# First group's two sets on raw, transposed x, with the normalisation put in afterwards

## The chip, the core and the metric

The kernel runs on one core of a Trainium2 chip. The metric is the device time of one execution in microseconds. The engines are TensorE (PE in the profile; PEld is its weight load), VectorE (DVE), ScalarE (ACT), GpSimd (POOL) and SyncE (SP, which issues nearly all DMAs). All arithmetic is in 32-bit floats.

## The reference

With `x` of 2 x 1024 tokens by 512 features:

```
xn  = (x - mean(x)) / sqrt(var(x) + 1e-5)                  # per token
s   = xn @ (weight * blockmask).T                          # 512 x 512, 32 x 32 blocks
nx  = xn * rsqrt(mean(xn^2) + 1e-5) * ln_w
ffn = (silu(nx @ gate.T) * (nx @ up.T)) @ down.T           # 1792 hidden features
out = x + s * silu(ffn)
```

## The kernel before

Tokens are split into four tiles of 512 (t = 0 to 3), the 512 features into four chunks of 128 (c = 0 to 3). The matrix products are done by a two-level recursive scheme (seven products in place of eight, on each level). On the outer level a group g of gate and up columns has seven sets q; its two first sets, q = 1 and q = 2, multiply the plain blocks of the weights (feature halves K = 0 and 1) by the plain blocks of token tiles 0 and 1. The program's `order` lists first q = 1 and 2 of every group (g = 0 to 7, where group 7 is the masked linear layer), then the other five sets of every group. Position j in this list numbers a set: j = 0 and 1 are group 0's two, j = 2 and 3 group 1's. The down projection follows with a similar scheme.

Each set is one call of `instance`: seven products, m = 1, 5, 2, 6, 3, 7, 4 in order of issue, each a 128x128 by 128x512 matmul (two records in the trace). Products 1, 2 and 3 take token blocks as they are, 5, 6, 7 and 4 take differences of token blocks, which `inner_b` makes: with b11, b12, b21, b22 for (chunk, tile) they are t5 = b12 - b11, t6 = b22 - t5, t7 = b22 - b12, t4 = b21 - t6. `inner_a` makes the sums of weight blocks on POOL, after `scale_a` has multiplied a weight tile by `ln_w`. Products accumulate in three kinds of PSUM banks, X (three banks), Y (two) and Z (one); a fourth kind, V (two), serves everything else: idle products, transposes, gate values, held copies. Banks of a kind are used in turn. Between products, a bank's running value is copied out (`snap`, `seed`, `total`): by ACT in a group's first set, by DVE with an addition of the first set's sums (`prior`) in its second. From j = 2 on a set is `seeded`: ACT copies X into the Z bank before product 2 accumulates there.

All instructions are put into one list with `at(pos, ...)` and issued in the order of `pos`; every engine carries out its own in that order. One position is one product slot, 7 per set; `T(us)` turns a planned time into a position. `plan` puts in a list of steps. The times in the program only set the order.

At the head, `load_x` loads x by tokens, `stats` and `factors` make each token's scale and shift, `normalise` applies them (ACT and DVE, in halves of 256 columns), `transpose` turns each 128x128 piece on TensorE into a V, X or Y bank, and `evacuate` copies it out. Products of set 0 need the transposed pieces of tile 0, the differences those of tile 1. Meanwhile `warm` runs 22 idle products on the identity. Tiles 2 and 3 are done otherwise, later: `load_xt` loads x already transposed (`x_t`), `fac_rows` turns the factors into rows through TensorE, writes them to DRAM and reads them back over all partitions, and `scale_xt` applies them on POOL.

`group` has where a group's sums go: `acc` for set 1's, `c1` for set 2's; when two halves of c1 are complete, `silu` (ACT) and `h_out` (DVE) make the gated product, and later an SP transfer stores the `acc` sums to DRAM.

Of the kernel before, what the change touches and what calls it, by code (L numbers as in the profile page):

```python
# [31 lines left out]
def tile_masked_linear_gated_ffn(  # L32
# [22 lines left out]
    fac_dram = tc.dram_tile([2, 2, W], F32, name="fac_dram")  # L55
# [51 lines left out]
    blockones = const.tile([P, P], F32, tag="blockones", name="blockones")  # L107
    keep = const.tile([P, 4, 16], F32, tag="keep", name="keep")

    def constants():  # L110
        nc.gpsimd.memset(eps2, EPS * EPS)
        make_identity(nc, ident)
        nc.scalar.activation(stat_0, eps2, AF.Sqrt)
        nc.gpsimd.memset(blockones, 0.0)
        for b in range(P // BLK):
            nc.gpsimd.memset(blockones[b * BLK : (b + 1) * BLK, b * BLK : (b + 1) * BLK], 1.0)
# [4 lines left out]
    fac = small.tile([P, 2, 2, TT], F32, tag="fac", name="fac", bufs=1)  # L121
    rms = small.tile([P, NTT, TT], F32, tag="rms", name="rms", bufs=1)

    def load_x(t):
        for i in range(TT):
            xt[t, i] = mem[:, first_slot[("B6", "vc", "v5", "B4")[t]] + i, :]
            nc.sync.dma_start(xt[t, i], x[(t * TT + i) * P : (t * TT + i + 1) * P, :])
# [6 lines left out]
    def factors(t, i=0, n=TT):  # L134


        if t < 2:
            scl = small.tile([P, n], F32, tag="scl", name=f"scl_{t}_{i}", bufs=3)
            nb = small.tile([P, n], F32, tag="nb", name=f"nb_{t}_{i}", bufs=3)
        else:  # L140
            scl, nb = fac[:, t - 2, 0, :], fac[:, t - 2, 1, :]
        for k in range(n):
            stat[t, i + k] = (scl[:, k : k + 1], nb[:, k : k + 1])
        rows = slice(i, i + n)

        def last():
            nc.vector.reciprocal(scl, scl)
            nc.vector.scalar_tensor_tensor(nb, agg[:, t, rows, 0], -1.0, scl, ALU.mult, ALU.mult)

        return [lambda: nc.scalar.activation(scl, agg[:, t, rows, 1], AF.Sqrt, bias=eps2, scale=1.0 + EPS), last]  # L150
# [60 lines left out]
    def fac_rows(t):  # L211
        b = bank("V", f"fac_rows_{t}")
        nc.tensor.transpose(b[: 2 * TT, :P], fac[:, t - 2].rearrange("p f i -> p (f i)"), ident)
        rows = small.tile([2 * TT, P], F32, tag="rows", name=f"fac_sb_{t}")
        nc.scalar.copy(rows, b[: 2 * TT, :P])
        nc.sync.dma_start(fac_dram[t - 2].rearrange("f (i p) -> (f i) p", p=P), rows)
        for f in range(2):
            fac_bc[t, f] = mem[:, F["B6"] + 3 + 2 * (t - 2) + f, :]
            nc.sync.dma_start(fac_bc[t, f], fac_dram[t - 2, f].unsqueeze(0).to_broadcast([P, W]))

    def scale_xt(t, c, f):
        v = u12[c, t % 2] if c < 2 else raw[c, t]
        add(pool, v, v, fac_bc[t, f], (ALU.mult, ALU.add)[f])

# [160 lines left out]
    def instance(j, g, q, prior, dest, after):  # L385
# [4 lines left out]
        seeded = j > 1  # L390

        def mm(m, tag, key, first):
            if first and key not in st:
                st[key] = bank("Y" if key == "z" and j == 1 else tag, f"{key}_{j}")
            nc.tensor.matmul(st[key], weights(g, q, m), operand(q, m), start=first and not (key == "z" and seeded),  # L395
                             stop=True, skip_group_check=True)

        def seed():

            if seeded:  # L400
                st["z"] = bank("Z", f"z_{j}")
                nc.scalar.copy(st["z"], st["x"])  # L402
            else:
                st["s1"] = slot("s2" if j else "s5", f"s1_{j}")
                if prior is None:
                    nc.scalar.copy(st["s1"], st["x"])
                else:
                    add(dve, st["s1"], st["x"], prior(0))
# [19 lines left out]
        for off, m, tag, first, snapshot, out in (  # L428
# [9 lines left out]
            at(EARLY.get((j, m), pos), mm, m, tag, key, first)  # L438
            if snapshot:
                at(pos + 1, snap, key, *snapshot)  # L440
            elif out:

                pos += 2.3 if prior is None and m == 2 and seeded else 1
                if m == 2:
                    pos = EARLY.get((j, "z"), pos)
                at(pos, total, key, *out)
# [3 lines left out]
    def group(g, where):  # L450
# [5 lines left out]
        h11 = tiles(F["a1"])  # L456
        gate = {}
# [14 lines left out]
        def done(R, Hh, tiles):  # L472
# [3 lines left out]
            def after(i, pos):  # L476
# [5 lines left out]
                if n in ready and n + 2 in ready:  # L482
                    key = (R, Hh, n)
                    p = max(ready[n] + 1.2, ready[n + 2] - 0.5, SILU)
# [5 lines left out]
        def summed(dst, src, into, then=None, engines=(pool,) * 4):  # L490
# [9 lines left out]
            1: (None, acc, nothing),  # L500
            2: (acc, c1, done(0, 0, c1)),
# [16 lines left out]
        at(7 * where[g, 1] + 15, lambda: nc.sync.dma_start(acc_dram[g], sums))  # L518
# [117 lines left out]
    def down_instance(o, q, where_, prior, dest, after):  # L636
# [78 lines left out]
        if last_set:  # L715
            at(where_(17) + 0.1, base_of_last)
            for part, pos in zip(parts, (where_(23), where_(24), where_(25))):
# [12 lines left out]
    EARLY.update({(0, 1): T(10.4), (0, 2): T(11.3), (1, 1): T(12.1), (1, 2): T(13.0), (0, 0): T(11.5), (1, 0): 4.3,  # L730
                  (0, "z"): 2.2, (1, "z"): 4.5})
    SILU = 26.2
    at(T(-10), constants)
    at(T(-10), load_x, 0)
    at(T(-10), lambda: nc.scalar.dma_start(lnw_sb, ln_w))

    at(T(-10), lambda: nc.gpsimd.tensor_copy(mem[:, F["a1"], 0:1], xt[0, 0][:, 0:1]))
    at(T(-10), load_a, 0, 0)
    at(T(-10), load_x, 1)
    at(T(-10), load_a, 0, 1)  # L740

    at(T(9.95), lambda: nc.gpsimd.memset(mem[:, F["a1"] + 2, 0:1], 0.0))
    for K in range(2):
        at(T(9.96), load_a, 1, K)
    at(T(9.96), load_x, 2)
    for K in range(2):
        at(T(9.96), load_a, 2, K)
    at(T(9.96), load_x, 3)
# [8 lines left out]

    at(T(1.4), lambda: warm(22, bank("V", "idle")))
    plan(T(4.9), 0, factors(0, 0, 2))
    plan(T(7.1), 0, factors(0, 2, 2))  # L760
    for t, p, step in ((1, T(12.5), 0), (3, 23.2, 0.6), (2, 36.1, 1.2)):
        plan(p, step, factors(t))
    for us, i, h in ((5.9, 0, 0), (6.0, 0, 1), (6.1, 1, 0), (7.2, 1, 1), (7.95, 2, 0), (8.4, 2, 1), (7.95, 3, 0), (8.4, 3, 1)):
        at(T(us), normalise, 0, i, dve if i == 3 else act, slice(h * W // 2, (h + 1) * W // 2))
    for i in range(TT):
        half = act if i < 2 else dve
        at(T(3.7 + 0.82 * i), stats, 0, i)
        at(T(9.35 + 0.82 * i), stats, 1, i)
        for h, cols in enumerate((slice(0, W // 2), slice(W // 2, W))):
            at(T(13.45 + 0.9 * h + 0.4 * (i % 2)), normalise, 1, i, half, cols)  # L770
        for c in range(KC):
            at(T((8.9, 9.3, 9.8, 11.0)[c] + 0.05 * i), transpose, 0, c, (0, 1, 3, 2)[i], "XYYX"[c])
            at((T(14.35), T(14.8), T(15.25), 4.1)[c] + 0.06 * i, transpose, 1, c, (2, 3, 0, 1)[i], "XVVV"[c])
    at(T(6.0), scale_a, 0, 0, pool)
    at(T(10.0), scale_a, 0, 1, pool)
    for c in range(KC):
        at(T((9.75, 10.3, 10.85, 12.05)[c]), evacuate, 0, c, act)
        at((5.6, 2.09, 6.0, 5.05)[c], evacuate, 1, c, act)
    for pos, q, m, eng in ((1.1, 1, 5, dve), (1.87, 1, 6, dve), (2.56, 1, 7, dve), (3.95, 2, 5, dve), (2.7, 1, 4, pool),
                           (5.06, 2, 6, dve), (10.05, 2, 7, dve), (5.07, 2, 4, pool)):  # L780
        at(pos, inner_b, q, m, eng)
    for q in (1, 2):
        for k in (0, 1):
            for n in (0, 1):
                at(8, outer_b, q, k, n, None)
    at(5.1, scale_a, 1, 0)
    at(5.2, scale_a, 1, 1)
    for i in range(TT):
        at(14.0 + 2.5 * i, stats, 3, i)
# [5 lines left out]
    at(25.2, fac_rows, 3)  # L795
    at(40.8, fac_rows, 2)
    for n, p0 in ((1, 31), (0, 50)):
# [3 lines left out]
    for k in (0, 1):  # L801
        at(37 + 1.5 * k, outer_b, 7, k, 1, pool)
        at(43 + 1.5 * k, outer_b, 6, k, 1, pool)
# [19 lines left out]
    for g in range(G + 1):  # L823
# [8 lines left out]
        if g:  # L832
            plan(p - 7, 1, inner_a(g, 1))
        else:
            plan(T(9.9), 0, inner_a(0, 1, 0, 1))
            plan(2.75, 0, inner_a(0, 1, 1, 1))
# [150 lines left out]
```

## Time and profile before

| | |
|---|---|
| median of 3 runs | 506.8 us (506.78 to 507.37) |
| the profiled execution | 506.61 us, span 504.8 us |
| TensorE busy | 499.2 us (99%) |
| VectorE busy | 375.6 us (74%) |
| ScalarE busy | 188.1 us (37%) |
| GpSimd busy | 358.8 us (71%) |
| DMA | 124.75 MB, mean 247 GB/s |

All times of a row are in microseconds from the span's start. A row of the view in order of time has the start, the time taken by the rows merged in it, the engine, the line, what is written and read, how many, and in brackets how long the engine sat idle before it and what released it. The chain is found from the end backwards: each instruction is followed to what it waited for. A busy share is an average over the whole span; the head and the rest of the kernel have different limits.

### The profile page before, as it was taken

What the parts mean: (1) busy time and instruction counts of PE and PEld (TensorE: products, weight loads), DVE (VectorE), ACT (ScalarE), POOL (GpSimd) and SP (SyncE); (2) the same over time, 40 slices, a digit from 0 to 9 for tenths busy, and PEclk for the clock granted to TensorE, in tenths of its full rate; (3) what the DMA queues carried; (4) which work ended last, traced back from release to release, by engine and by line L of the source; (5) the groups of instructions that cost most, each with busy time, mean ns of one, the idle gap of its engine ahead of it and who ended that gap; (6) DMA issues with size and microseconds to landing.
All of it is one profiled execution on the core that took longest, in us unless ns stands there. A gap on an engine that the chain in (4) does not pass through costs nothing.

```text
span 504.8 us, 4923 instructions
## 1 busy us (share of the span) xinstructions
PE 499.2 (99%) x1231; PEld 227.4 (45%) x1231; DVE 375.6 (74%) x578; ACT 188.1 (37%) x362; POOL 358.8 (71%) x301
## 2 busy tenths in 40 slices
PE   8999999999999999999999999999999999999996
PEld 7444444444444444444444444444444444444444
DVE  6887887876968969697896969879657644377636
ACT  6667775734535363443535333330101101001111
POOL 5629997464886959879696999985672764649960
PEclk9999999999999999999999999999999999999999
DMA  6878746368178594876949475599996798467362
GB/s 208 306 234 335 292 168 250 123 251 293 62 245 295 186 329 181 295 240 244 335 154 317 179 265 213 216 351 387 365 335 221 253 389 311 130 238 269 106 229 84
DMA packets 62221, 124.75 MB, mean 247 GB/s; under 512 B 5968, under 2 KB 13552, under 8 KB 60144
## 3 DMA queue, kind: packets, MB, share of 16 engines
q1 hardware_dynamic: 62048, 124.43, 69.1%
q8 instruction: 10, 0.16, 0.1%
q14 instruction: 19, 0.16, 0.1%
q10 hardware_dynamic: 144, 0.00, 0.0%
HBM read 78.25 MB, written 46.15 MB: 246 GB/s over the span
## 4 chain that ended last, share of the span: by engine, by line
PE 97%; DVE 1%; ACT 1%; DMA 1%; issue 0%; DVEq 0%; ACTq 0%
PE x L395 38%; PE y L395 19%; PE dx L643 15%; PE z L395 10%; PE dy L643 8%; PE dz L643 5%; PE dv L643 1%; PE pt L165 1%; DMA mem<-in_x 1%; DVE mem L98 0%; ACT mem L158 0%; DVE st L131 0%; DVE mem L633 0%; ACT silu L626 0%; ACT scl L150 0%
## 5 line engine op out<-in xcount | busy, mean ns | idle before, releaser
L98 POOL TENSOR_TENSOR mem<-mem 128x512 f32<-128x512 f32 (+4 forms) x261 | 322.1, 1257 | 111.6 <-ACT mem L423 30.5
L395 PE MATMUL x<-mem 128*128 128x512 f32 x448 | 211.7, 593 | 0.0
L395 PEld LDWEIGHTS x<-mem 128*128 128x128 f32 x448 | 84.6, 190 | 107.3 <-issue 89.7
L98 DVE TENSOR_TENSOR mem<-x,mem 128x512 f32<-128x512 f32 x137 | 93.4, 686 | 42.1 <-PE x L395 40.4
L395 PE MATMUL y<-mem 128*128 128x512 f32 x224 | 114.6, 593 | 0.1
L643 PE MATMUL dx<-mem 128*128 128x512 f32 x174 | 78.3, 592 | 0.0
L98 DVE TENSOR_TENSOR mem<-mem 128x1536 f32<-128x1536 f32 (+3 forms) x50 | 66.9, 1342 | 6.9 <-PE dx L643 4.4
L98 DVE TENSOR_TENSOR mem<-y,mem 128x512 f32<-128x512 f32 x96 | 65.9, 686 | 7.9 <-PE y L395 6.5
L402 ACT COPY z<-x 128x512 f32<-128x512 f32 x54 | 30.9, 573 | 94.7 <-PE x L395 91.7
L395 PEld LDWEIGHTS y<-mem 128*128 128x128 f32 x224 | 42.2, 190 | 53.1 <-issue 46.5
L395 PE MATMUL z<-mem 128*128 128x512 f32 x112 | 57.3, 593 | 0.0
L643 PEld LDWEIGHTS dx<-mem 128*128 128x128 f32 x174 | 33.1, 190 | 41.6 <-issue 40.9
L643 PE MATMUL dy<-mem 128*128 128x512 f32 x98 | 44.5, 592 | 0.0
L461 ACT ACTIVATE gate<-mem 128x512 f32<-128x512 f32 x56 | 32.7, 602 | 20.4 <-DVE mem L98 15.9
L466 DVE TENSOR_TENSOR mem<-gate,mem 128x512 f32<-128x512 f32 x56 | 38.1, 682 | 1.9 <-ACT gate L461 1.5
L616 POOL TENSOR_TENSOR mem<-mem 128x512 f32<-128x512 f32 x16 | 25.8, 1619 | 13.6 <-DMA mem<-s_dram 13.4
L626 ACT ACTIVATE silu<-mem 128x512 f32<-128x512 f32 x15 | 9.0, 602 | 64.6 <-DVE mem L98 48.3
L395 PEld LDWEIGHTS z<-mem 128*128 128x128 f32 x112 | 21.1, 190 | 25.9 <-issue 21.4
L98 DVE TENSOR_TENSOR mem<-z,mem 128x512 f32<-128x512 f32 x41 | 28.1, 685 | 2.8 <-PE z L395 2.7
L643 PEld LDWEIGHTS dy<-mem 128*128 128x128 f32 x98 | 18.6, 190 | 23.4 <-issue 23.2
L98 DVE TENSOR_TENSOR mem<-dx,mem 128x512 f32<-128x512 f32 x16 | 11.1, 691 | 20.3 <-PE dx L643 20.2
L643 PE MATMUL dz<-mem 128*128 128x512 f32 x56 | 25.2, 592 | 0.0
(86 smaller groups left out, 286.9 us busy)
## 6 DMA issues: line engine op xcount, KB each, us to landing
h_dram<-mem SPq DMA_DIRECT2D x98, 256.0 KB, 2.2
mem<-h_dram SPq DMA_DIRECT2D x28, 768.0 KB, 6.7
mem<-in_gu SPq DMA_DIRECT2D x42, 256.0 KB, 3.9
acc_dram<-mem SPq DMA_DIRECT2D x8, 1024.0 KB, 4.0
mem<-acc_dram SPq DMA_DIRECT2D x8, 1024.0 KB, 6.1
mem<-in_x_t SPq DMA_DIRECT2D x24, 256.0 KB, 5.5
mem<-in_x SPq DMA_DIRECT2D x16, 256.0 KB, 4.5
s_dram<-mem SPq DMA_DIRECT2D x16, 256.0 KB, 6.1
```

The lines of the kernel that those rows point to most:

```text
L98: eng.tensor_tensor(o, a, b, op)
L165: nc.tensor.transpose(pt[t, c][:, i * P : (i + 1) * P], xt[t, i][:, c * P : (c + 1) * P], ident)
L395: nc.tensor.matmul(st[key], weights(g, q, m), operand(q, m), start=first and not (key == "z" and seeded), stop=True, skip_group_check=True)
L402: nc.scalar.copy(st["z"], st["x"])
L461: nc.scalar.activation(gate[key], t(), AF.Silu)
L466: nc.vector.tensor_mul(a(), gate[key], b())
L616: at_later.append(lambda: nc.gpsimd.tensor_tensor(s_tile, s_tile, rms_bc[t], ALU.mult))
L626: nc.scalar.activation(b[0][:, part], y[:, part] if source is None else source(), AF.Silu)
L643: nc.tensor.matmul(st[key], w(), b(), start=first and key != "z", stop=True, skip_group_check=True)
```

## The change

Sets 0 and 1 (group 0, q = 1 and 2) no longer wait for normalised tokens. They multiply raw x, loaded already transposed (`load_rx`); `raw_b` makes their differences, on DVE through a copy in a V bank (`rhold`) or on POOL. Since normalising is a scale and a shift for each token, and a token is a column of the outputs, the outputs are mended: `mend_scale` multiplies by the tokens' scale, `mend_shift` adds the tokens' shift times the sum of the weights over features. These sums are made by `row_sums`, eight products with a column of ones. The factors of tiles 0 and 1 go through `fac_rows` as those of 2 and 3 do; `hold_fac` copies such a tile into a V bank for DVE. Tile 0 and 1 are still normalised and transposed, for group 1 onwards, and what belonged to j = 0 and 1 in the order's early part (the use of tile 1's transposes, the unseeded sets) moves on by 14 positions (S) to j = 2 and 3. Group 0's sums lie in other slots (`acc_1`, `c1` in B3 and B4), its `silu` comes at position 39.5, its store at 53. The number of idle products goes from 22 to 17, loads are issued in another order, and two small POOL instructions that held back weight loads go.

```diff
+    def load_rx(c, t):
+        i = {0: F["B5"] + 3, 1: F["B5"] + 5, 2: F["B5"], 3: F["B7"]}[c] + t
+        rx[c, t] = mem[:, i, :]
+        nc.sync.dma_start(rx[c, t], x_t[c, t])
...
+    def rhold(c):
+        rheld[c] = bank("V", f"rx_{c}")
+        nc.scalar.copy(rheld[c], rx[c, 1])
...
+        if eng is dve:
+            a, b = (rheld[c], rx[c, 0]) if m == 5 else (rheld[c + 1], rop[q, 5])
+        else:
+            a, b = (rx[c + 1, 1], rx[c, 1]) if m == 7 else (rx[c + 1, 0], rop[q, 6])
+        add(eng, o, a, b, ALU.subtract)
+
+    def row_sums():
+        b = bank("V", "row_sums")
+        for K in range(2):
+            for r in range(2):
+                for c in range(2):
+                    nc.tensor.matmul(b[:, 2 * K + r : 2 * K + r + 1], aq[0, 0, K][:, (2 * c + r) * P :][:, :P], ones,
+                                     start=c == 0, stop=c == 1, skip_group_check=True)
+        nc.vector.tensor_copy(rowsum[:, 0, :], b[:, 0:2])
+        nc.vector.tensor_tensor(rowsum[:, 1, :], b[:, 2:4], rowsum[:, 0, :], ALU.add)
...
+    def hold_fac(n, f):
+        fac_held[n, f] = bank("V", f"fac_{n}_{f}")
+        nc.scalar.copy(fac_held[n, f], fac_bc[n, f])
+
+    def mend_scale(v, n, eng):
+        add(eng, v, v, fac_held[n, 0] if eng is dve else fac_bc[n, 0], ALU.mult)
+
+    def mend_shift(v, k, r, n):
+        nc.vector.scalar_tensor_tensor(v, fac_held[n, 1], rowsum[:, k, r : r + 1], v, ALU.mult, ALU.add)
...
-        seeded = j > 1
+        seeded = j > 3
...
+            nc.tensor.matmul(st[key], weights(g, q, m), rop[q, m] if j < 2 else operand(q, m), start=first and not (key == "z" and seeded),
...
+            for n in range(2):
+                for r in range(2):
+                    at(23.6 + 1.2 * (2 * n + r), lambda n=n, r=r: mend_scale(c1(2 * r + n), n, pool))
+                    at(34.5 + 2.6 * n + 0.9 * r, lambda n=n, r=r: mend_shift(c1(2 * r + n), 1, r, n))
+                    at(44 + 4.4 * n + 0.9 * r, lambda n=n, r=r: mend_scale(acc_1(2 * r + n), n, dve))
+                    at(46 + 4.4 * n + 0.9 * r, lambda n=n, r=r: mend_shift(acc_1(2 * r + n), 0, r, n))
+                at(33.5 + 2.6 * n, hold_fac, n, 1)
+                at(43 + 4.4 * n, hold_fac, n, 0)
+                at(45 + 4.4 * n, hold_fac, n, 1)
...
-                    p = max(ready[n] + 1.2, ready[n + 2] - 0.5, SILU)
+                    p = max(ready[n] + 1.2, ready[n + 2] - 0.5, SILU if g else 39.5 + 0.5 * n)
...
+    for j, todo in enumerate((
+        {1: 4.9, 2: 5.8, 5: 6.7, 6: 7.6, 3: 8.5, 7: 9.4, 4: 11.1, 0: 6.6, (5, "out"): 7.7, (6, "out"): 8.5, (2, "out"): 9.3,
+         (3, "out"): 10.0, (7, "out"): 10.5, (4, "out"): 12.0},
+        {1: 10.2, 2: 12.0, 5: 12.9, 6: 13.8, 3: 14.7, 7: 15.6, 4: 18.0, 0: 11.1, (5, "out"): 14.55, (6, "out"): 14.8,
+         (2, "out"): 14.1, (3, "out"): 16.2, (7, "out"): 16.4, (4, "out"): 19.0})):
...
-    at(T(-10), load_x, 0)
...
     at(T(-10), load_a, 0, 0)
+    for c, t in ((0, 0), (1, 0), (0, 1), (1, 1)):
+        at(T(-10), load_rx, c, t)
+    at(T(-10), load_x, 0, 0, 2)
+    at(T(-10), load_a, 0, 1)
+    at(T(-10), load_rx, 2, 0)
+    at(T(-10), load_x, 0, 2, 4)
+    for c, t in ((3, 0), (2, 1), (3, 1)):
+        at(T(-10), load_rx, c, t)
+    at(T(-10), load_a, 1, 0)
     at(T(-10), load_x, 1)
+    at(T(-10), load_a, 1, 1)
...
-    at(T(1.4), lambda: warm(22, bank("V", "idle")))
-    plan(T(4.9), 0, factors(0, 0, 2))
-    plan(T(7.1), 0, factors(0, 2, 2))
+    at(T(1.4), lambda: warm(17, bank("V", "idle")))
+    plan(T(9.25), 0, factors(0, 0, 2))
+    plan(T(14.5), 0, factors(0, 2, 2))
...
+    for us, i, h in ((10.5, 0, 0), (10.6, 0, 1), (11.1, 1, 0), (11.2, 1, 1), (15.2, 2, 0), (15.3, 3, 0), (15.35, 2, 1), (15.4, 3, 1)):
+        at(T(us), normalise, 0, i, act, slice(h * W // 2, (h + 1) * W // 2))
...
+            at(T(16.6 if c < 2 else 18.05) + 0.1 * c + 0.01 * i, transpose, 0, c, (0, 1, 3, 2)[i], "VVXX"[c])
+            at((T(14.35), T(14.8), T(15.25), 4.1)[c] + 0.06 * i + S, transpose, 1, c, (2, 3, 0, 1)[i], "XVVV"[c])
+    at(T(3.6), scale_a, 0, 0)
+    at(T(9.1), scale_a, 0, 1)
+    at(T(13.0), scale_a, 1, 0)
+    at(T(17.0), scale_a, 1, 1, pool)
+    for us, c in ((5.6, 0), (6.3, 1), (11.8, 2), (12.5, 3)):
+        at(T(us), rhold, c)
+    for us, q, m, eng in ((6.1, 1, 5, dve), (6.8, 1, 6, dve), (7.0, 1, 7, pool), (8.9, 1, 4, pool), (12.4, 2, 5, dve),
+                          (13.2, 2, 6, dve), (13.3, 2, 7, pool), (15.1, 2, 4, pool)):
+        at(T(us), raw_b, q, m, eng)
+    at(9.6, row_sums)
+    at(5.4, fac_rows, 0)
+    at(15.4, fac_rows, 1)
```

## The prediction

> **What bounds the kernel now.** I read the page first (busy shares and the chain that ended last), then the TensorE and ScalarE rows of the first 30 us in order of time, then busy time by stretch where the change puts its repairs.
>
> ```profile
> PE 499.2 (99%) x1231; PEld 227.4 (45%) x1231; DVE 375.6 (74%) x578; ACT 188.1 (37%) x362; POOL 358.8 (71%) x301
> PE 97%; DVE 1%; ACT 1%; DMA 1%; issue 0%; DVEq 0%; ACTq 0%
> ```
>
> The chain is TensorE at 97%: 392 products of the first phase and then the down phase, at one product per 0.858 us (1.72 us for two in the chain's rows). Time can be won only by starting the stream earlier or by closing gaps in it; any gap that the change opens is lost in full. So the head decides:
>
> ```profile
> 1.37 6.97 PE L756 MATMUL idle<-ident 128*128 128x128 f32 x44 [1.37 <-POOL ident masks.py:199]
> 8.78 1.39 PE L165 MATMUL pt<-ident,mem 128*128 128x128 f32 x10 [0.22 <-DVE mem L156]
> 10.01 1.10 PE L395 MATMUL x<-mem 128*128 128x512 f32 x2
> 14.31 1.47 PE L165 MATMUL pt<-ident,mem 128*128 128x128 f32 x12
> 15.69 1.13 PE L395 MATMUL y<-mem 128*128 128x512 f32 x2
> 22.58 1.02 PE L395 MATMUL y<-mem 128*128 128x512 f32 x2
> ```
>
> The 22 idle products are 44 records and keep TensorE until about 8.06. The first real product starts at 10.01; the one at 22.58 is the twelfth, and from there products follow without a gap. Eleven products are 9.44 us, so 12.57 us hold 3.1 us of something else: 20 transposes at 0.11 (2.2 us) and 0.9 us of gaps. The head is nearly full already.
>
> Two rows show a bank that TensorE waits for:
>
> ```profile
> 14.95 1.49 DVE L98 TENSOR_TENSOR mem<-pt,mem 128x512 f32<-128x512 f32 x2 [0.46 <-PE pt L165]
> 16.47 0.58 ACT L173 COPY mem<-pt 128x512 f32<-128x512 f32 x1 [1.29 <-DVE mem L98]
> 17.11 0.14 PEld L165 LDWEIGHTS pt<-ident,mem 128*128 128x128 f32 x1 [0.26 <-ACT mem L173]
> ```
>
> Two V banks are used in turn. V banks go to the idle products, then to tile 1's chunks c=1, c=2, c=3. So c=3 must wait for the copy of c=1, which ends at 17.05; its weights load at 17.11. Here two products lie ahead of it and hide the wait.
>
> **The change, part by part.** I write (j, m) for product m of set j; sets 0 and 1 are those that now take raw x.
>
> *Start: the gain.* Busy time by half microseconds shows the idle products' pace change near 5.0 to 5.2 us (some 4 records touch a stretch before, 6 to 7 after, though the granted clock reads 1.00 throughout). From there 28 of the 44 records remain, 3.0 us, 0.107 each; the first 16 took 3.7 us. Now there are 17 products, 34 records: 16 before 5.1, then 18 x 0.107 = 1.9, so TensorE is free at 7.0. Is the data there? Ten loads of 256 KB landed between 3.5 (the first) and about 10.05 (the DMA share falls from 0.97 to 0.04 at 10), 0.73 apart. In the new order the weight tile lands first, 3.5; x_t chunks at 4.2, 5.0, 5.7, 6.5; the scaling on ACT takes 0.9, done by 4.6. The idle products end last: (0,1) starts at 7.06, 2.95 earlier than before. [...]
>
> *Sets 0 and 1: a new queue on ACT.* ACT's rows follow program order. Its steps: copy 0.48, scaling one weight tile 0.88, four normalise halves 2.08. A reader of a product starts 1.14 after the product does (10.01 to 11.15). (0,6) is the fourth product, 9.63; its snapshot starts on ACT at 10.77; the second weight tile's scaling is behind it, 11.25 to 12.13. (1,1) needs that and starts at 12.26, (1,2) at 13.98. But ACT then has the square root (0.3), a 0.45 wait for DVE's factors, and four normalise halves, 13.0 to 15.1, before it copies the x_t chunk that (1,5)'s operand is taken from: 15.1 to 15.7. DVE, one statistics pair of 0.82 in its way, subtracts at 16.1 to 16.8. (1,5) starts at 16.85, where TensorE was free at 14.84: **gap 2.0**. ACT goes on: two copies, the next weight tile (to 17.4), the square root that waits for the fourth x tile's statistics (DVE, 18.2), factors, four more halves 19.24 to 21.35. TensorE ends (1,7) at 20.29 and its next work, the transposes of tile 0, needs the halves: **gap 1.2**.
>
> *Row sums and the factor rows.* Eight products with one output column are 16 records. None is in the trace; by the transposes (0.107 a record, the same 128-column weights) 1.7 us, 1.4 by the 0.087 load of the fac_rows row, 3.0 by the 0.19 load of the products. I take 1.7. In the order they stand just ahead of (2,1), so they are on the path; a gain is excluded, since nothing is taken away for them. Two more fac_rows transposes add 0.24. [...]
>
> So: transposes of two chunks 0.9, (1,4) 0.86, two chunks 0.9, factor row and sums 1.8 after 21.45: (2,1) starts at 25.9; four products later, 29.4, tile 1's transposes.
>
> *The bank.* New V banks (two held chunks twice, two transposes, fac_rows of tile 0, row sums) come first, and fac_rows of tile 1 falls between chunks c=1 and c=2. Now c=2 falls on c=1's bank and is queued ahead of (2,5). By the rows above the bank comes free 2.1 after DVE's first subtraction starts (14.95 to 17.05). TensorE has nothing to do meanwhile: transposes end at 30.4, c=2 starts at 32.0, **gap 1.6**, and (2,5) at 32.47. It is the nineteenth product; before, the nineteenth is at 22.58 + 7 x 0.858 = 28.59, and c=3's 0.45 lies behind it only now. The terms: -2.95 (start), +1.3 (twelve transposes that lay ahead of the first product before), +2.0, +1.2, +1.7, +0.2, +1.6, less before's own 0.9 of gaps: +4.2, by the two clocks 32.47 + 0.45 - 28.59 = **+4.3**. [...]
>
> *Repairs on DVE.* Between positions 33 and 52 come 8 shifts and 4 scalings of 128x512 on DVE, 6 copies on ACT, and two gate products are moved there: 14 DVE operations at 0.60 (start to start of full rows) = 8.4 us. The shift's form is not in the trace at this size; the bank-reading row it is nearest to takes 0.68, 0.60 in a stream; half or double are the ends. This is before's 43 to 59 us; the rows give busy time by stretch, in the order TensorE, weight loads, DVE, ACT, POOL:
>
> ```profile
> 46.00:50.00 4.00, 4.00 (x12) 1.75 (x11) 2.33 (x5) 1.95 (x4) 4.00 (x5) 1.00 0.97 372
> 50.00:54.00 4.00, 4.00 (x11) 1.75 (x10) 2.54 (x5) 3.99 (x9) 4.00 (x4) 1.00 0.49 154
> 54.00:58.00 4.00, 4.00 (x10) 1.71 (x9) 3.90 (x7) 2.42 (x6) 3.18 (x5) 1.00 1.00 380
> 58.00:62.00 4.00, 4.00 (x11) 1.68 (x10) 3.91 (x8) 2.30 (x5) 4.00 (x5) 1.00 0.75 298
> ```
>
> DVE idles 1.67 and 1.46 in the first two and 0.1 in each of the last two; with 1.1 in 42 to 46 that is some 4.2 up to 54. So 8.4 - 4.2 leaves DVE 4.2 late at position 52. Who waits: the one Z bank. DVE's total of z at 59.22 frees it at 59.9; ACT's seed of the next z starts at 60.77, and TensorE needs it about 1.0 after the seed ends. Slack 0.9 + 1.0 = 1.9, so 4.2 late costs TensorE 2.3, say **+2.4** with the copies that wait for V banks in the same queue. Ends 0 (double slack, or shorter shifts) and +5.
>
> *At nothing:* four scalings on POOL (4 x 1.07) lie where POOL idled 6.1 us for factor rows (33 to 39 us); if they ran over, POOL's sums would be late by the rest. SP now waits for two more factor rows, and behind these stand mask, weight and x_t loads that are used over 8 us later. The store of the first group's sums moves to position 53, behind the last shift; its load back is at 106.
>
> **Sum.** 4.3 + 2.4 = 6.7. The profiled execution took 506.61 (span 504.8 and 1.8 around it), 0.2 below the median of 506.8: 513.3 from the one, 513.5 from the other. I say **513.4**.
>
> **Rivals.**
> *Faster: ACT keeps the order's own times.* If (0,1) starts near 5 and the copy for (1,5) is on ACT before 13.0, both ACT gaps (3.2) go and, with the start, another 1.6 to 2.0; if the repairs fit into DVE's idle time, the sum is 4.3 - 3.2 - 2 = -0.9, and to -2.5 if the bank also comes free in time: about 505. For it: the loads land early enough. Against: snapshots, two weight tiles and eight halves stand in one queue, and the idle products alone hold TensorE to 7.0. It decides at (1,5): under 13.6 this rival, over 16 mine. 0.15.
> *Only the head costs.* DVE's backlog meets more slack than one seed row shows: 506.8 + 4.3 = 511. 0.25.
> *Backlog and bank feed each other.* ACT's held copies wait for V banks that a late DVE holds, so seeds come later than DVE itself: +5 in place of 2.4, 516. 0.10.
> *It cancels.* [...] 0.10.
> *Mine,* 0.40; alone it spans 511 to 516.
>
> Faster by over 0.2% (1 us, about what a measurement can tell): the first rival and a little of the fourth, 0.16; within it 0.06; slower 0.78. Leaving out the first rival and the tail over 518, the range is 506 to 518.
>
> **What would show it.** Right: the first product at about 7.0; (1,5) 1.5 to 2.5 late, with its ACT copy behind normalise rows; 16 narrow records of 1.4 to 2 us in all; c=2's transposes waiting for an ACT copy; DVE without idle time from 45 to 68 us, and a TensorE gap behind a late z seed near 60 to 70. Wrong: products at one per 0.858 from 5 us on, or TensorE without gaps after 35.

## The result, and the profile after

| | before | after |
|---|---|---|
| median | 506.93 us (506.78 to 507.37) | 527.69 us (525.03 to 528.97) |
| ratio after/before | | 1.0401 [1.0361, 1.0442] |
| profiled execution | 506.61, span 504.8 | 525.03, span 523.2 |
| TensorE busy | 499.2 | 503.7 |
| VectorE busy | 375.6 | 387.4 |

The kernel became 20.8 us slower; 513.4 had been forecast, with a range of 506 to 518. The profiled execution is the fastest of the four and lies 2.7 under the median, so the traces below hold 18.4 of the 20.8.

The page's busy shares and the shares of the chain that ended last:

```profile
PE 503.7 (96%) x1239; PEld 227.9 (44%) x1239; DVE 387.4 (74%) x596; ACT 194.7 (37%) x376; POOL 367.0 (70%) x310
PE 83%; DVE 1%; ACT 0%; issue 0%; DVEq 0%
```

TensorE has 8 records more, for 4.5 us more of busy time; the span grew by 18.4. So some 14 us more are time in which TensorE waits. Its rows in order of time, from the head:

```profile
7.36 1.02 PE L442 MATMUL x<-mem 128*128 128x512 f32 x2
14.90 1.10 PE L442 MATMUL x<-mem 128*128 128x512 f32 x2 [1.23 <-DVE mem L98]
16.91 1.10 PE L442 MATMUL y<-mem 128*128 128x512 f32 x2
20.32 1.10 PE L442 MATMUL y<-mem 128*128 128x512 f32 x2 [1.24 <-POOL mem L98]
25.07 1.84 PE L255 MATMUL row_sums<-ones,mem 128*128 128x1 f32 x16
31.78 0.66 PE L164 MATMUL pt<-ident,mem 128*128 128x128 f32 x4 [0.34 <-ACT fac_sb L214]
32.27 1.02 PE L442 MATMUL y<-mem 128*128 128x512 f32 x2
```

The head is close to what was forecast: first product 7.36 (7.06), (1,5) at 16.91 (16.85), row sums to the next work 1.70 (1.7), (2,5) at 32.27 (32.47). Behind the head come three waits, of which only the last has a place in the forecast:

```profile
37.55 1.02 PE L442 MATMUL x<-mem 128*128 128x512 f32 x2
44.00 0.37 PE L212 MATMUL fac_rows<-ident,fac 128*8 128x128 f32 x1 [5.42 <-DVE fac L147]
44.17 1.92 PE L442 MATMUL x<-mem 128*128 128x512 f32 x2
45.87 1.45 PE L442 MATMUL y<-mem 128*128 128x512 f32 x2
...
61.88 0.27 PE L212 MATMUL fac_rows<-ident,fac 128*8 128x128 f32 x1 [3.40 <-DVE mem L529]
...
72.86 1.12 PE L442 MATMUL z<-mem 128*128 128x512 f32 x2 [1.26 <-ACT z L449]
```

A convenient measure is the lateness of the n-th product: its start in the profiled execution minus the start of the n-th product in that of before. It counts waits and added work together and needs no account of them. Products 19, 23, 27, 43 and 59 stand behind the head, ahead of tile 3's `fac_rows` in `after`, behind it, behind tile 2's `fac_rows`, and behind the wait for the Z seed. (The lines below the first are runs told of further down.)

| | median us | ratio [95%] | n=19 | 23 | 27 | 43 | 59 |
|---|---|---|---|---|---|---|---|
| after | 527.69 | 1.0401 [1.0361, 1.0442] | 3.7 | 4.6 | 11.6 | 15.2 | 17.9 |
| e1 | 522.86 | 1.0318 [1.0298, 1.0337] | 4.1 | 5.0 | 7.9 | 12.3 | 15.0 |
| e2 | 525.12 | 1.0360 [1.0344, 1.0375] | 3.6 | 4.5 | 11.5 | 13.3 | 16.9 |
| e3 | 521.76 | 1.0298 [1.0283, 1.0313] | 4.2 | 5.1 | 8.1 | 10.6 | 15.1 |
| e4 | 519.73 | 1.0261 [1.0242, 1.0281] | 3.4 | 4.3 | 10.7 | 11.9 | 11.9 |
| e7 | 519.50 | 1.0253 [1.0238, 1.0268] | 4.2 | 5.1 | 5.9 | 8.3 | 12.8 |
| e10 | 520.47 | 1.0267 [1.0250, 1.0284] | 3.7 | 4.6 | 5.4 | 8.1 | 13.3 |
| e9 | 517.40 | 1.0217 [1.0199, 1.0236] | 1.5 | 3.0 | 3.8 | 5.9 | 9.9 |
| e8 | 526.95 | 1.0397 [1.0374, 1.0420] | 2.6 | 3.5 | 10.9 | 16.7 | 19.4 |
| e11 | 517.88 | 1.0216 [1.0200, 1.0231] | 3.8 | 5.1 | 5.0 | 7.5 | 11.1 |
| e12 | 512.60 | 1.0113 [1.0098, 1.0128] | 3.4 | 4.7 | 4.6 | 4.7 | 5.2 |
| e13 | 518.22 | 1.0222 [1.0205, 1.0239] | 3.6 | 4.9 | 4.8 | 7.6 | 11.2 |
| e14 | 512.06 | 1.0103 [1.0086, 1.0120] | 2.5 | 3.8 | 3.7 | 3.8 | 4.3 |

In `after`, 4.6 is lost by product 23, 7.0 between 23 and 27, 3.6 up to 43 and 2.7 up to 59; nothing much later. Two cautions go with the table. A row's lateness holds the chance of its start (the first product begins between 6.76 and 7.90 with 17 idle products), so differences along a row are surer than those between rows. And the median of `after` lies 2.7 above its profiled run, so gains over `after` are larger by medians than by lateness at product 59: e1 4.8 and 2.9, e2 2.6 and 1.0, e3 5.9 and 2.8, e7 8.2 and 5.1, e11 9.8 and 6.8.

The 7.0 is the largest, and it stands at an instruction that the change moved by only 0.4 positions: `at(25.6, fac_rows, 3)`, 25.2 before. It needs tile 3's factors from DVE. VectorE's rows in order of time:

```profile
30.93 1.49 DVE L98 TENSOR_TENSOR mem<-pt,mem 128x512 f32<-128x512 f32 x2 [2.33 <-PE pt L164]
...
40.57 0.68 DVE L134 BATCH_NORM_STATS2 st<-mem 128x6 f32<-128x512 f32 x1
...
42.55 0.17 DVE L146 RECIPROCAL fac<-fac 128x4 f32<-128x4 f32 x1
42.76 1.10 DVE L147 SCALAR_TENSOR_TENSOR fac<-agg,fac 128x4 f32<-128x4 f32 x1
```

The first of these is tile 1's differences, which need its transposes. They began at 14.95 before and begin at 30.93 now, because their transposes moved on by 14 positions (S). Tile 3's statistics (positions 17.5 to 22.6, before 14.0 to 21.5), factors (23.9, before 23.2) and `fac_rows` (25.6, before 25.2) moved too, in lines that the diff above leaves out, but by 3.5 positions at most. What DVE had 24 positions for, from the first difference to `fac_rows`, now lies in ten, in one queue, so the reciprocal that ran at 32.80 before runs at 42.55. The rows of before:

```profile
32.80 0.14 DVE L147 RECIPROCAL fac<-fac 128x4 f32<-128x4 f32 x1
32.98 0.16 DVE L148 SCALAR_TENSOR_TENSOR fac<-agg,fac 128x4 f32<-128x4 f32 x1
33.74 0.27 PE L213 MATMUL fac_rows<-ident,fac 128*8 128x128 f32 x1
```

The last DVE row of `after`, 1.10 us for 128 x 4 numbers, took 0.16 before. POOL is scaling for the repairs at that time, and the two end within 0.03 us of each other (43.83 and 43.86):

```profile
42.57 1.26 POOL L98 TENSOR_TENSOR mem<-mem 128x512 f32<-128x512 f32 x1
```

In e4, which leaves the repairs out, this DVE row takes 0.16 again and TensorE's wait is 4.49 in place of 5.42:

```profile
42.50 0.16 DVE L147 SCALAR_TENSOR_TENSOR fac<-agg,fac 128x4 f32<-128x4 f32 x1
42.81 0.37 PE L212 MATMUL fac_rows<-ident,fac 128*8 128x128 f32 x1 [4.49 <-DVE fac L147]
```

The repairs on DVE begin only at 53.59, so some 0.94 of the wait goes with those on POOL; the rest is DVE's order.

The wait costs more than its length, which busy time by stretch of `after` shows (TensorE, weight loads, DVE, ACT, POOL, then granted clock, DMA share and GB/s):

```profile
38.00:42.00 4.00, 0.58 (x2) 0.00 (x0) 3.90 (x10) 0.30 (x1) 3.84 (x6) 1.00 0.98 370
42.00:46.00 4.00, 2.00 (x4) 1.00 (x5) 3.20 (x7) 0.25 (x1) 4.00 (x4) 0.66 0.32 120
46.00:50.00 4.00, 4.00 (x10) 1.74 (x9) 2.16 (x4) 2.35 (x3) 0.28 (x1) 0.91 0.63 134
```

After 5.4 us without work the granted clock is 0.66 and then 0.91, as means of 4 us; inside them it is 0.50 from 43.3 to 46.7 and 1.00 otherwise (last section). The two products behind the wait start 1.70 and 1.29 apart (44.17, 45.87, 47.16) in place of 0.858, which adds 0.84 + 0.43 = 1.3 us. Waits of the same length differ in this, as rows in the last section show. DVE waits 2.33 us before 30.93 and then never stops until 45: its order, not its mean load, is what TensorE meets.

POOL is hit too, through the same factors, which it gets by way of DRAM. The first row is POOL's first scaling of tile 3 before, the second the same one after:

```profile
39.10 15.08 POOL L98 TENSOR_TENSOR mem<-mem 128x512 f32<-128x512 f32 x14 [6.13 <-DMA mem<-fac_dram]
```

```profile
50.67 2.51 POOL L98 TENSOR_TENSOR mem<-mem 128x512 f32<-128x512 f32 x2 [4.39 <-DMA mem<-fac_dram]
```

The second wait has another cause. Group 0's gate activations now sit at 39.5 and 40.0, in V banks, just ahead of tile 2's `fac_rows` at 40.8, and their bank comes free only when DVE has multiplied with the gate:

```profile
53.59 0.75 DVE L270 SCALAR_TENSOR_TENSOR mem<-fac,rowsum,mem 128x512 f32<-128x512 f32 x1 [0.38 <-ACT fac L264]
...
61.15 1.27 DVE L529 TENSOR_TENSOR mem<-gate,mem 128x512 f32<-128x512 f32 x2
```

L529 is the multiplication by the gate, L270 the first shift. TensorE's row at 61.88 above names this multiplication as what ended its wait of 3.40.

### The profile page after: what moved, and what is told of

The parts are those of the page before. It is cut to its first block, busy times and chain, and to the rows that moved or that the text cites. A ratio compares the mean times of both kernels' runs of the same rounds, so it can differ in the third digit from the quotient of the medians.

```text
span 523.2 us, 5019 instructions
## 1 busy us (share of the span) xinstructions
PE 503.7 (96%) x1239; PEld 227.9 (44%) x1239; DVE 387.4 (74%) x596; ACT 194.7 (37%) x376; POOL 367.0 (70%) x310
## 4 chain that ended last, share of the span: by engine, by line
PE 83%; DVE 1%; ACT 0%; issue 0%; DVEq 0%
PE x L442 32%; PE y L442 16%; PE dx L707 14%; PE dy L707 8%; PE z L442 8%; PE dz L707 5%; PE dv L707 1%; DVE mem L98 1%; DVE mem L697 0%; ACT silu L690 0%; DVE mask_sums L399 0%; PE pm L403 0%; PE rms_rows L189 0%; DVEq L697 0%; DVEq L98 0%
## 5 line engine op out<-in xcount | busy, mean ns | idle before, releaser
L98 POOL TENSOR_TENSOR mem<-mem 128x512 f32<-128x512 f32 (+4 forms) x273 | 332.8, 1242 | 126.8 <-DVE mem L98 39.4
L449 ACT COPY z<-x 128x512 f32<-128x512 f32 x52 | 29.8, 573 | 94.1 <-PE x L442 91.1
L529 DVE TENSOR_TENSOR mem<-gate,mem 128x512 f32<-128x512 f32 x56 | 38.1, 681 | 1.3 <-ACT gate L524 1.0
L707 PE MATMUL dz<-mem 128*128 128x512 f32 x56 | 25.2, 592 | 0.0
```

Source lines behind the costliest of these rows:

```text
L98: eng.tensor_tensor(o, a, b, op)
L529: nc.vector.tensor_mul(a(), gate[key], b())
L707: nc.tensor.matmul(st[key], w(), b(), start=first and key != "z", stop=True, skip_group_check=True)
```

## The experiments

All kernels below are edits of `after`.

**The two `fac_rows` waits and the repairs.** Is the 7.0 us only the wait of an instruction that stands too early (the place of `fac_rows`), or a lateness of DVE that is met anyway?

e1:

```diff
-    at(25.6, fac_rows, 3)
+    at(32.4, fac_rows, 3)
```

> fac_rows of tile 3 goes from position 25.6 to 32.4, nothing else. Queue theory: TensorE's 5.6 us at 38.4 to 44.0 is lost only because a 0.1 us transposition that waits for DVE's factors stands ahead of products that are ready; put behind six more products it waits for nothing, and the 5.6 us and the slow clock after them (1.3 us) come back: about 520 us in place of 527.7 (profile 525.0 to about 518.5). Backlog theory: DVE is short of time from 31 us on, so products that need its sums wait in the transposition's place: at most 2 us come back, 525 or more, and TensorE shows two or three new waits on DVE between 38 and 50 us.

Measured 522.86, 4.8 less. The wait of 5.42 and the slow clock behind it are gone (the mean granted clock of the profile is 0.998, that of `after` 0.995), but TensorE now waits for additions of DVE at three products:

```profile
41.09 1.12 PE L442 MATMUL x<-mem 128*128 128x512 f32 x2 [2.13 <-DVE mem L98]
42.57 1.10 PE L442 MATMUL y<-mem 128*128 128x512 f32 x2 [0.36 <-DVE mem L98]
45.00 1.10 PE L442 MATMUL x<-mem 128*128 128x512 f32 x2 [0.47 <-DVE mem L98]
```

The first two lie between products 23 and 27, where lateness grows by 3.0 (7.0 in `after`). Each theory is half right: moving the reader saves the clock and part of the wait, while DVE's squeeze still costs 3.0.

e2 moves group 0's gates behind tile 2's `fac_rows`:

```diff
-                    p = max(ready[n] + 1.2, ready[n + 2] - 0.5, SILU if g else 39.5 + 0.5 * n)
+                    p = max(ready[n] + 1.2, ready[n + 2] - 0.5, SILU if g else 41.5 + 0.5 * n)
```

> Group 0's two gate activations go from positions 39.5 and 40.0 to 41.5 and 42.0, behind fac_rows of tile 2 (40.8), nothing else. Queue theory: TensorE's 3.6 us at 58.3 to 61.9 is a wait for a V bank that the gate values hold until DVE has read them; with the gates behind the transposition it only waits for DVE's factors (58.8 in the profile), so 2.5 to 3.3 us come back: about 524.7 median. Backlog theory: DVE's lateness reaches TensorE by the Z bank instead, and under 1 us comes back.

Measured 525.12, 2.6 less. TensorE's gap at that `fac_rows` fell from 3.56 to 0.51, and lateness at product 43 by 1.9. The V bank held by the gates is the cause; what is left of the wait is for tile 2's factors:

```profile
58.74 0.27 PE L212 MATMUL fac_rows<-ident,fac 128*8 128x128 f32 x1 [0.35 <-DVE fac L147]
```

Not all of it is won: the next product now waits 0.98 for DVE, the Z seed's wait grows from 1.26 to 1.85, and by product 59 only 1.0 is left in the profile. The first wait is unchanged (11.5 at 27).

e3 is e1 and e2 together.

> Both moves at once. Queue theory: the gains add, 9 to 10 us, about 517.5; what is left over before is the head (4.1) and the Z-bank waits behind the repairs (2.7) and part of the moved waits, 514 to 518. Backlog theory: less than 4 us, 523 or more.

Measured 521.76: 5.9 less, not the sum of 7.4. A reader that is moved later moves its own followers: tile 3's rows reach POOL later still, and POOL's first scaling has gone from 50.67 to 56.79:

```profile
56.79 18.48 POOL L98 TENSOR_TENSOR mem<-mem 128x512 f32<-128x512 f32 x18 [9.96 <-DMA mem<-fac_dram]
```

So neither single move is the remedy. (Whether the missing 1.5 lies there is not shown; the runs of e1 have mean granted clocks of 0.992 to 1.000, those of e2 of 0.993 to 0.996.) The four runs of e3 are within 0.7 us (521.5 to 522.2) with a mean granted clock of 0.998 to 1.000; those of `after` spread over 3.9 at 0.986 to 0.995. The fastest run of `after`, the profiled one, is at 0.995 and the other three at 0.986 to 0.988; e8's profile, at 0.988, has two slow stretches where that of `after` has one (last section). Whether the slow clock makes the spread is not shown.

e4 leaves out the repairs (no scaling, no shift, no held factors; the first group's sums stay as raw x gives them):

```diff
-            for n in range(2):
+            for n in range(0):
                 for r in range(2):
                     at(23.6 + 1.2 * (2 * n + r), lambda n=n, r=r: mend_scale(c1(2 * r + n), n, pool))
```

> Leaves out the repairs: no mend_scale, no mend_shift, no hold_fac, so group 0's outputs stay unscaled; everything else of the change stays. If the repairs cost what the prediction priced (2.4) or the 2.7 us of Z-bank and V-bank waits after 70 us that the profile shows, 525; if their load on DVE is also why fac_rows of tile 2 waits (four shifts lie ahead of the gates' products), another 2.5, 522 to 523. The 5.6 us at fac_rows of tile 3 stays in every case, since it ends before the first repair on DVE (53.6 us).

Measured 519.73: 8.0 less, more than any theory gave. Three things went at once: the first wait fell to 4.49, as told above; without shifts ahead of it in DVE's queue the gate's bank comes free sooner (lateness 43: 11.9, not 15.2), and nothing is lost behind 43. As part of e4's gain lies at the first wait and the gates' bank, it isn't the price of the repairs alone.

**DVE's order.** e7 is e3 with tile 3's statistics spread into the head and tile 2's put later:

```diff
-        at(17.5 + 1.7 * i, stats, 3, i)
-        at(23.5 + 2.8 * i, stats, 2, i)
+        at((14.95, 14.97, 17.5, 19.2)[i], stats, 3, i)
+        at(24.6 + 2.4 * i, stats, 2, i)
```

> e3 (both moves) with DVE's statistics moved too: two of tile 3's four go from positions 17.5 and 19.2 to 14.95, into the 2.3 us that DVE idles before tile 1's transposes, and tile 2's four start behind tile 3's factors (24.6, 2.4 apart, in place of 23.5, 2.8 apart). If what is left of the gap at 38 to 45 us in e3 (3.5 us in three waits for DVE) is DVE's work squeezed into 10 positions, 2 x 0.82 of it go, 2.5 with the pair of tile 2: about 519.5 in place of 521.8. If those waits come from something else than the amount of DVE's work there (ACT's or POOL's order), nothing changes: 521.5 to 522.

Measured 519.50, as the squeeze theory had it, and 2.3 less than e3. From product 23 to 27 it loses 0.8, where e3 loses 3.0: the order of the statistics on DVE was most of the rest of the squeeze.

e10 is e7 without the repairs:

> e7 without the repairs (no mend_scale, mend_shift, hold_fac: group 0's outputs stay unscaled). In e4 leaving them out took away the waits after 62 us, 4 to 6 us of TensorE's lateness. Here the wait at fac_rows of tile 2 is gone already, so 3.5 to 4 us: about 516, and nothing is lost any more behind 46 us. If the repairs and the late gates only shared one loss, under 2 us: 518.

Measured 520.47, a miss: no gain at all over e7 (519.50). From product 23 to 27 it loses 0.8, as e7 does, and by product 42 it is 6.1 late, so DVE's squeeze is no worse; but `fac_rows` at 32.4 still starves POOL, and now that shows:

```profile
54.32 21.61 POOL L98 TENSOR_TENSOR mem<-mem 128x512 f32<-128x512 f32 x21 [12.88 <-DMA mem<-fac_dram]
```

POOL idles for 12.88 us, then has 21 operations queued. TensorE waits 1.91 for POOL ahead of product 43 and 2.73 for DVE ahead of product 53; lateness goes to 13.3 by 59. Of that, 1.8 is a slow clock behind the second wait: products 53 to 56 start 1.29, 1.71 and 1.37 apart in place of 0.858. The factors of tile 3 have two readers, TensorE and POOL; an earlier chain would serve both, which e11 tries.

e9 is e10 without `row_sums` and `fac_rows` of tiles 0 and 1:

```diff
-    at(9.6, row_sums)
-    at(5.4, fac_rows, 0)
-    at(15.4, fac_rows, 1)
```

> e10 without row_sums and without fac_rows of tiles 0 and 1 (raw sets with nothing to mend them). By the profile row_sums keep TensorE from 25.07 to 26.77, 1.7, and the two transpositions 0.1 to 0.6 with the bank wait: 1.9 to 2.3 less than e10, about 514. What remains over before is then the head's own waits and DVE's squeeze. Rival: TensorE would wait for DVE in their place, since DVE sets the pace from 31 us: under 1 less.

Measured 517.40: 3.1 less than e10, more than the 1.9 to 2.3 of TensorE's own time. Lateness at 19 fell by 2.2, at 23 by 1.6; the rest comes later, where the wait for POOL is 0.6 shorter and the slow clock of e10's profile is missing, so this run doesn't price the sums; e14 comes nearer.

e8 is `after` with 8 idle products:

```diff
-    at(T(1.4), lambda: warm(17, bank("V", "idle")))
+    at(T(1.4), lambda: warm(8, bank("V", "idle")))
```

> The changed kernel with 8 idle products in place of 17, nothing else. If the idle products alone hold the first product to 7.4 (as the prediction had it), it starts near 4.9, and runs at the slow pace until about 5; the operands of the third and fourth product are ready at 7.7 and 9.1 by the profile, where these started at 9.07 and 9.93, so the head gains 0.8 to 1.4 and the whole 0.5 to 1.5: about 526.5. [...]

Measured 526.95, 0.7 less and within the spread of `after`: inconclusive as a time. In the profile the first product starts at 4.95 (7.36), and of these 2.4 us 1.1 are left at product 19 (2.6 late, not 3.7). Tile 3's `fac_rows` waits for DVE as long as in `after` (5.43), 1.1 earlier; but the clock is slow for longer behind it, and slow again behind tile 2's `fac_rows` (last section), so that product 43 is 16.7 late, not 15.2.

**The chain moved as a whole.** e11 puts tile 3's statistics, factors and `fac_rows` ahead of tile 1's differences, and keeps e2's gates and e7's statistics of tile 2:

```diff
-    for t, p, step in ((1, T(19.7), 0), (3, 23.9, 0.6), (2, 36.3, 1.2)):
+    for t, p, step in ((1, T(19.7), 0), (3, 15.5, 0.38), (2, 36.3, 1.2)):
...
-        at(17.5 + 1.7 * i, stats, 3, i)
-        at(23.5 + 2.8 * i, stats, 2, i)
+        at(14.95 + 0.01 * i, stats, 3, i)
+        at(24.6 + 2.4 * i, stats, 2, i)
...
-    at(25.6, fac_rows, 3)
+    at(16.25, fac_rows, 3)
```

> The changed kernel with tile 3's factors brought forward: all four of its statistics at position 14.95, before tile 1's differences, its square root at 15.5, its factors at 15.88 and its fac_rows at 16.25 (17.5 to 25.6 before); tile 2's statistics from 24.6 on; group 0's gates at 41.5 as in e2. Chain theory: what e3, e7 and e10 left over is one chain, tile 3's factors, their rows in DRAM, POOL's scaling of tile 3, which began at 39.1 in the kernel before, at 50.7 in the changed one and at 54 to 57 in e3, e7 and e10. Here POOL begins at 39 to 43; left over are the head (5), some 1 us by which tile 1's differences come later, and the repairs (2.4 to 5): 514 to 518, 516 likeliest. Amount theory: DVE has too much work between 28 and 45 us in any order, 519 to 521 as e7.

Measured 517.88: 9.8 less than `after`. Nothing is lost between product 23 and 27, and POOL no longer waits for a transfer:

```profile
37.39 24.23 POOL L98 TENSOR_TENSOR mem<-mem 128x512 f32<-128x512 f32 x23 [0.95 <-DVE mem L98]
```

This row begins with other work. POOL's first scaling of tile 3 stands in it behind the repairs' four scalings and starts at 46.52: later than the 39 to 43 expected, but 4.2 earlier than in `after`.

The first losses behind the head are now at tile 2's `fac_rows` and the product behind it, and then at a Z seed, all behind DVE's repairs; from the list of TensorE's waits in e11 (us in total, how often, longest):

```profile
PE z L442 <- ACT z L449: 1.8, 1, 1.8
PE y L442 <- DVE mem L98: 0.9, 1, 0.9
PE fac_rows L212 <- DVE fac L147: 0.9, 1, 0.9
```

e12 is e11 without the repairs (the edit of e4). With the chain in its better place, no long wait for POOL or for tile 3's factors hides what they cost.

> e11 without the repairs (no mend_scale, mend_shift, hold_fac: group 0's outputs stay unscaled). In e10 leaving them out gained nothing, because POOL was late by itself. By the chain theory POOL is in time here, so that the repairs' own price shows, as in e4: 2.4 (as predicted) to 5 us less than e11, about 513. By the amount theory no gain, as in e10.

Measured 512.60: the repairs cost 5.3. Product 59 is 5.2 late, of which 4.7 stem from the head. From the list of TensorE's waits in e12:

```profile
PE y L442 <- POOL mem L98: 1.2, 1, 1.2
PE x L442 <- DVE mem L98: 1.2, 1, 1.2
PE pt L164 <- ACT fac_sb L214: 0.3, 1, 0.3
PE z L442 <- ACT z L449: 0.2, 1, 0.2
```

The first three lie in the head, ahead of (1,3), (0,4) and (2,5), as in `after`. With the repairs gone, the Z seed's wait went from 1.8 to 0.2, and the two waits at tile 2's `fac_rows` are no longer in the list.

**The head.** e13 is e11 with the head's order smoothed around its two waits of 1.4 us: the copies of raw x for set 1's differences earlier, the factors of tile 0 on DVE, its last statistics and its first normalising later.

```diff
-    plan(T(9.25), 0, factors(0, 0, 2))
-    plan(T(14.5), 0, factors(0, 2, 2))
+    plan(T(9.25), (10.6 - 9.25) / 0.86, factors(0, 0, 2))
+    plan(T(15.0), 0, factors(0, 2, 2))
...
-    for us, c in ((5.6, 0), (6.3, 1), (11.8, 2), (12.5, 3)):
+    for us, c in ((5.6, 0), (6.3, 1), (9.3, 2), (11.25, 3)):
```

> e11 with the head's order changed: the held copies for sets 1's differences go ahead of tile 0's normalising on ACT (9.3 and 11.25 in place of 11.8 and 12.5), DVE's first factors behind set 0's totals (10.6 for 9.25), and the fourth tile's statistics and factors behind the snapshots of set 1 (14.9 and 15.0 for 14.0 and 14.5). If the two gaps of 1.43 and 1.47 in the head are DVE's and ACT's order, as the profile's releasers say, they shrink below 0.5 each; tile 0's normalising comes up to 1 us later, so 1 to 2.5 less than e11: about 514.5. Rival: the gap moves to tile 0's transposes, within 0.5 of e11.

Measured 518.22, no gain over e11 (517.88). The two gaps of 1.43 and 1.47 became four of 0.30, 0.68, 0.45 and 0.29, and TensorE then waits 1.4 for tile 0's normalised halves (ACT): product 23 is 4.9 late, not 5.1. This edit of the order moved the head's waits and did not remove them.

e14 is e12 without `row_sums` and the two `fac_rows` (the edit of e9), so that no part of the mending is left.

> e12 without row_sums and without fac_rows of tiles 0 and 1: raw sets 0 and 1 with nothing at all to mend them, so the least that the idea can cost in this order. The sums' 16 records take 1.7 us of TensorE in every profile, the two transpositions and the wait for their bank 0.6; if TensorE alone sets the head's end, 2.0 to 2.3 less than e12, 510.4. If tile 0's and 1's normalising on ACT and DVE sets it, 1 or less comes back: 511.6 or more. In neither case is it under the kernel before.

Measured 512.06, 0.5 less than e12 (their intervals overlap). Lateness fell by 0.9 in the profiles, not by the 1.9 of TensorE's time that was taken away; (2,5) now waits 1.28 for DVE. So most of the row sums' time would otherwise be waited out just behind them.

No run beat the kernel before. Even with nothing to mend and the chain in its better place, the raw sets' head is 5.1 us slower (512.06 against 506.95 beside it).

## Why the prediction was wrong

The sum was 4.3 for the head and 2.4 for the repairs, 6.7. The runs give 20.8 as 9.8 (`after` to e11), 5.3 (e11 to e12) and 5.6 (e12 to the kernel before beside it, 507.0); by lateness at product 59 it is 17.9 as 6.8, 5.9 and 5.2.

**The missed step, 9.8.** The prediction costed what moves (tile 1's transposes and differences, 14 positions on) only where TensorE transposes. It did not ask what DVE work stayed close behind them. Tile 3's statistics and factors stand in no sentence of it, and its factor rows only as what POOL waited for before; the sum, which has no term between (2,5) at 32.47 and the repairs, failed at 38.4, where TensorE stopped. The rows to read were in the profile before: DVE's differences at 14.95 and tile 3's reciprocal at 32.80, 17.9 us apart. S is 14 products of 0.858, 12.0 us, and with the forecast head of 4.3 the differences move by 16.3 (15.98 in fact). A reciprocal that stayed at 32.80 would have 1.6 us left for DVE's work between the two, which took 11.6 in `after` (30.93 to 42.55). So the factors come some 10 us later than before; TensorE is 4.3 later itself, and 5.7 are left as a wait. The 5.42 measured is made of slightly other terms: the reciprocal came 9.75 later and TensorE 4.6, before had a slack of 0.6 (factors done at 33.14, `fac_rows` at 33.74), which makes some 4.5, and the rest is the 0.94 that DVE's last step lost beside POOL. All but the 11.6 stood in the profile before, and the 11.6 could have been summed: 13 additions at 0.60 and 5 statistics at 0.80, both from the rows of before, are 11.8. e1, e3 and e10 show that moving `fac_rows` alone is not enough; e11 shows 9.8 when the whole chain moves, with the gates' bank (2.6 by e2 alone) and the slow clock in it. How the 9.8 divides among the three stays open, since they overlap (e3: 5.9 for 4.8 and 2.6).

**The bank.** The prediction moved the gates to 39.5 as "two gate products are moved there" and counted only DVE's time for them. That they hold a V bank which `fac_rows` of tile 2 needs, 3.4 us of wait, was left out, though the same text had found such a wait at c=2. There it was wrong in the other way: c=2 waited 0.34, not 1.6, and for ACT's copy of tile 1's factor rows, not for c=1's. By these rows c=2 got the bank of tile 1's factor rows, free at 31.72, while c=1's was copied out only from 32.45; so V banks were not handed out strictly in turn, as the prediction had it.

**Repairs: 5.3 in place of 2.4,** just over the upper end of 5. The mechanism held for part of it: DVE was late, ACT's Z seed behind it, TensorE at the seed (72.86 in `after`, 1.8 in e11, 0.2 without repairs in e12). Between products 23 and 59 e11 loses 6.0 and e12 0.5. Of the 6.0, 2.0 are lost at the Z seed, near the 2.4 forecast, and 2.2 at tile 2's `fac_rows` and the product behind it, where the forecast had no term; the rest is in small pieces. Two terms of the sum were too small. The shift takes 0.74 where 0.68 was assumed, some 0.06 x 8 = 0.5 in all. And the cover, 4.2 us of idle DVE time, could be used only in part. Between the starts of products 34 and 52, before, in e11 and in e12:

```profile
41.58:57.14 15.56, 15.56 (x38) 6.86 (x37) 11.19 (x20) 11.39 (x22) 14.82 (x16) 1.00 0.87 331
46.66:67.02 20.36, 16.75 (x39) 6.51 (x37) 18.99 (x32) 15.81 (x30) 17.83 (x18) 1.00 0.85 321
46.24:62.36 16.12, 15.91 (x38) 6.76 (x37) 12.65 (x22) 13.10 (x25) 16.12 (x16) 1.00 0.84 323
```

DVE idles 4.4 us there before, 3.5 in e12 and 1.4 in e11, so the repairs filled 2.1 of it. Most of what they left in e11 is DVE waiting for ACT, 0.76 for the first held copy and 0.36 for a square root. The prediction wanted DVE without idle time from 45 to 68; in `after` it idles 1.84 in 46 to 50 alone, before the repairs on it begin (53.59). Of the rivals, the one in which backlog and bank feed each other has the mechanism of the seed's wait (in `after` ACT's held copy at 71.72 waits 0.93 for DVE, the seed at 72.25 right behind it) and about the size of the whole (5), but no term for the 2.2 at tile 2's `fac_rows`.

**Head: 4.6 by product 23, 5.2 by product 59 in e12, 5.6 by medians, against 4.3.** The size held, and (1,5) decided as the prediction said it would (16.91, over 16). The terms are partly luck. The forecast was one gap of 2.0 at (1,5) and one of 1.2 at the transposes. In fact (0,4) lost 1.43 behind DVE's total of (0,7) in its own X bank, DVE having waited for the factors that ACT had queued; (1,3) lost 1.47, by my reading behind DVE's snapshot of (1,5) in its Y bank, which ends at 20.22; the row at 20.32 names POOL, but the POOL sums that (1,3) needs were done by 15.63. The others lost 0.2 each. Sum of the four 3.3 against 3.2, and nothing was lost at the transposes of tile 0. ACT's queue is the common cause that the prediction named, but the reader that met it was another. The row sums took 1.70 (25.07 to 26.77), 0.107 a record, as by the transposes' row. In e13 they took 1.70 as well (24.85 to 26.55), and no profile shows them shorter. In time they cost, with the two factor rows, about 0.5 (e12 to e14, whose intervals overlap; 0.9 by lateness), since a wait lay beneath.

**The start:** 7.36 against 7.06, a difference within its scatter: over the twelve profiles with 17 idle products the first product starts between 6.76 and 7.90. The start near 5 for which the first rival counts 1.6 to 2.0 is in none of them; only with 8 idle products (e8) does the first product start at 4.95.

**What stood at nothing:** the two new factor rows on SP cost nothing that a row shows. POOL's four scalings did: 0.94 us of DVE's time at tile 3's factors in `after`, and in e11 they stand ahead of tile 3's scaling in POOL's queue. The POOL idle time that was to hide them (33 to 39) was itself an effect of waiting for tile 3's rows, and that wait went on to 50.67.

## What to carry to other kernels

When a step is moved back in a hand-written order, list for every engine what stays close behind it and add up that queue: a step that the diff moves by 0.4 positions may turn out to be the one that TensorE meets. A small instruction that waits in TensorE's queue (here one 128 x 8 transpose) stops a whole stream, and the stop can be paid a second time in clock (here 5.42 us, and 1.3 us behind it). When a late chain has two readers, move the chain, not a reader: moving one reader and the gates gave 5.9 (e3), moving the chain and the gates, with statistics of tile 2, 9.8 (e11).

## What was not expected of the hardware

- In or behind some long waits the granted clock was 0.50 for 3.3 to 3.4 us, once for 6.8 us, and then 1.00 again. Waits of the same length differ in this. With 5.42 us in `after` (to 44.00) it was 0.50 from 43.3 to 46.7, with 5.43 us in e8 (to 42.91) from 41.1 to 47.9. After 3.40 us in `after` (to 61.88) it stayed at 1.00; after 3.41 us in e8 (to 61.93) it was 0.50 from 61.6 to 64.9; after only 2.73 us in e10 (to 69.53) it was 0.50 from 70.2 to 73.5, and after 2.72 us in e9 (to 67.30) the next products start 0.96 and 0.86 apart (in e10 1.29 and 1.71). The first row is the one of `after` behind 3.40; the others are slow stretches of `after`, of e8 (two) and of e10:

```profile
62.00:66.00 4.00, 4.00 (x11) 1.85 (x11) 2.94 (x6) 2.30 (x5) 4.00 (x4) 1.00 0.27 56
43.31:46.73 3.42, 2.73 (x5) 1.21 (x6) 1.93 (x4) 0.84 (x2) 2.97 (x3) 0.50 0.04 12
41.10:47.90 6.80, 4.99 (x7) 2.22 (x8) 4.18 (x8) 0.84 (x2) 4.09 (x4) 0.50 0.48 176
61.60:64.90 3.30, 2.97 (x5) 1.42 (x6) 1.72 (x4) 1.21 (x3) 3.30 (x3) 0.50 0.02 7
70.20:73.50 3.30, 3.30 (x6) 1.40 (x5) 3.15 (x6) 1.08 (x2) 3.22 (x4) 0.50 0.35 146
```

  What sets the clock at these places is not shown.
- The row sums' matmuls (128 x 128 weights in 32-bit floats, a single output column) took 1.70 us for 16 records in `after` (25.07 to 26.77), some 0.11 us each; its transposes of 128 columns took as long (8 records in 0.87 us, 30.29 to 31.16).
